# Two memory pools change places: the token sorting's tiles and the attention's weights under the recurrence's buffers

## The chip, the cores and the metric

The kernel runs on one core of a Trainium2 chip. The metric is the device time of one execution in microseconds (us), lower is better; of several runs the median is taken. The core has five engines that work side by side, each through its own instructions in a fixed order: TensorE (PE in the profile, with its weight loads as PEld), VectorE (DVE), ScalarE (ACT), GpSimd (POOL) and SyncE (SP), which here only issues DMA transfers. POOL issues the indirect DMAs (gathers and scatters of rows) and some accumulating ones. An engine waits at an instruction until the semaphores that it needs are there, and all that stands behind it on this engine waits too.

## The reference, cut to what matters

A network of four layers on x of 4 x 1024 x 128 (batch B = 4, tokens T = 1024, features D = 128), float32 throughout. After every part there is an addition of the input and a layer norm.

```
layer 0: minGRU (two levels), then a feed-forward part that goes through 64 slots
layer 1: sparse attention of 16 heads, then a gated feed-forward part
layer 2: linear attention with 16 heads of 64 (cosformer), causal;
         then experts: each token goes to its best 2 of 8
             hidden = silu(x W1[e]) * (x W3[e]);  y = sum over the 2 of p_e * (hidden W2[e])
layer 3: a selective recurrence (Mamba): 256 channels, 16 states n each
             h_n(t) = exp(delta(t) A_n) h_n(t-1) + delta(t) u(t) B_n(t)
             y(t)   = sum over n of C_n(t) h_n(t)
         then 8 experts with top-p weights: every expert is computed for every token
```

## The kernel before, in words

The program builds layer after layer (`program`, L2161 on), but a scheduler of the tile framework orders each engine's instructions over all of it: the kernel states operations and their data, the framework plans the order with its own model of costs (`TileContext(nc, schedule_with_timeline_sim=True)`) and inserts the waits. Only TensorE's order within the attention of layer 2 is written by hand (`l2_attn`), and the recurrence is put ahead of the experts of layer 2 by a raised priority (`l3`).

**Pools.** Tiles live in pools, and pools lie on two stacks, one from the left and one from the right end of each partition's memory. A pool that is opened gets the space next to the pool opened before it on its side; when it's closed, a later pool may lie over it. The first tiles of such a later pool wait until all tiles of every older pool under it have been released. This is counted by the whole pool: a tile that lies over a pool waits for that pool's last user. On the right side stand, from the end inwards, `moek` (kept values), `first`, `moet` (the experts' weights, rows and results of layer 2), and then, within the `ExitStack` called `w2`, the pool `w2` (the attention's weights wE with the constants turn, near, trig and biases) and `moed` (work tiles of the token sorting). When `w2` is closed, three pools are opened: `ssm` and `ssm2` on the left (`l3_pools`, L1679), which hold the recurrence's buffers, and `top` on the right, which holds the last layer's expert weights wh and results.

**Attention of layer 2** (L903 to L1206). TensorE projects, rotates (POOL's qt at L1059) and sums by groups of 128 tokens; its last matmul is pr (L1196, with wE), and its last norm is written by VectorE at L178 (xN).

**Token sorting** (`l2_dispatch`, L1294). For each of the four batches VectorE turns the router's ranks into target rows: prefix sums, comparisons, an index di for each choice (L1361 to L1367), a weight wt (last operation L1377). Then POOL scatters the tokens' rows to memory outside the chip: 16 indirect DMAs a batch (L1383).

**Experts of layer 2** (`l2_ffn`, L1402). The sorted tokens are worked on in 92 tiles of 128, 23 a batch, m0 to m91 here. For each tile SP loads its expert's weights wx (L1458) and its rows xg (L1442); TensorE computes ph, ScalarE and VectorE the gating (L1490 to L1494), TensorE py; ScalarE copies ys (L1510), SP stores yrows (L1512). When a batch is done, POOL gathers its rows back as yg (L1529, 16 indirect DMAs, in two halves of 8), and a norm ends the layer.

**Recurrence of layer 3** (`l3_prepare` L1718, `l3_scan` L1819). It goes over eight halves of 512 tokens (four batches, two halves each), numbered 0 to 7 here. `l3_prepare` computes xs, the rows B and C, dl (delta) and ud (delta times u, L1813) of a half. Then, for each state n from 0 to 15:

```
...
                nc.sync.dma_start(
                    out=t[:, 0, :], in_=rows[r : r + 1, :].to_broadcast([P, 512])
                )
...
            nc.gpsimd.tensor_mul(db, ud, bc[0])
...
            nc.gpsimd.tensor_mul(hc, db, bc[1])
```

SP loads the rows bn and cn to all partitions (L1844); POOL multiplies db = ud x bn (L1849); ScalarE forms da = exp (L1853); VectorE runs two scans along the tokens in place in db (L1854); ScalarE keeps the last column as carry in a first half (L1863); POOL multiplies hc = db x cn (L1865); TensorE adds hc into pys by a matmul with the identity (L127). bn, cn, db and hc have four buffers each, all in `ssm2`. When all 16 are summed, `l3_sum` and `l3_finish` (po, the norm, the router) end the half, and `l3_ffn_head` (first pgt, L1944 on) and the 8 experts of the last layer (`l3_ffn`, weights wh loaded by SP at L1677) follow for it, while POOL, VectorE and ScalarE go on with the next half.

The pools and their places in KB of a partition, before and after the change:

| pool | holds | before | after |
|---|---|---|---|
| `ssm2` (left) | bn, cn, db, hc, xnT, xs, dl, ud, tail, carry | 76.31 to 152.62 | the same |
| `moed` (right) | work tiles of the sorting | 146.81 to 156.00 | 175.88 to 185.06 |
| `w2` (right) | wE and constants of the attention | 156.00 to 185.06 | 146.81 to 175.88 |
| `top` (right) | h_acc, gT, wh, hh | 155.06 to 185.06 | the same |
| `moet` (right) | the experts' tiles of layer 2 | 185.06 to 217 | the same |

Of the kernel before, what the change touches and what calls it, by code (L numbers as in the profile page):

```python
# [49 lines left out]
def weave(*gens):  # L50

    gens = list(gens)
    while gens:
        for g in gens[:]:
            if next(g, gens) is gens:
                gens.remove(g)
# [2104 lines left out]
def program(tc, io):  # L2161
    with ExitStack() as ctx:
        n = Net(ctx, tc, io)
        wd, w0 = ExitStack(), ExitStack()
        wdp = wd.enter_context(tc.tile_pool(name="wd", bufs=1))
        W = n.l0_load(w0.enter_context(tc.tile_pool(name="w0", bufs=1)))
        d = n.l1_ffn_load(wdp)
        dp = ctx.enter_context(
            tc.tile_pool(name="rows", bufs=2, space=bass.MemoryType.DRAM)
        )  # L2170
        sd = ctx.enter_context(tc.tile_pool(name="ssmd", bufs=2, space=bass.MemoryType.DRAM))
        with ExitStack() as ff:
            last = n.front(ff, w0, W, d, dp)
            keep = ctx.enter_context(tc.tile_pool(name="moek", bufs=1, side="right"))
            first = ctx.enter_context(tc.tile_pool(name="first", bufs=1, side="right"))
            mt = ctx.enter_context(tc.tile_pool(name="moet", bufs=2, side="right"))
            w2 = ExitStack()
            n.l2_attn_load(w2.enter_context(tc.tile_pool(name="w2", bufs=1, side="right")))
            weave(*last)
        wd.close()  # L2180
        def load():
            n.l2_ffn_load()
            n.l3_load(sd)
            n.l2_rows(keep, md, dp)

        moe = n.l2_ffn(mt)
        with w2:
            md = w2.enter_context(tc.tile_pool(name="moed", bufs=1, side="right"))
            n.l2_attn(load, n.l2_dispatch, moe, first)
        n.l3_pools(ctx)  # L2190
        fp = ctx.enter_context(tc.tile_pool(name="top", bufs=2, side="right"))
        n.l3(moe, fp)
# [17 lines left out]
```

## Time and profile before

| what | us |
|---|---|
| runs | 2287.27, 2288.26, 2295.73; median 2288.26 |
| the profiled execution | 2286.79, its span 2285.0 |
| busy PE / DVE / ACT / POOL | 1978.9 / 1349.2 / 1210.5 / 1023.4 |
| attention's last pr, last norm L178 ends | 1339.7, 1345.5 |
| last operation of the last sorting (L1377) ends | 1371.4 |
| the recurrence's first bn issued, first db | 1371.5, 1390.3 |
| last hc of half 0 ends, its po begins | 1476.3, 1482.3 |
| last layer: first pgt, first expert's ph | 1545.7, 1549.1 |
| last db of the recurrence | 2134.9 |

The profile shows one execution. Its page gives busy times, the span in 40 equal slices (each digit is the busy share in tenths; PEclk is TensorE's granted clock in tenths of full speed), the chain of work that ended last, and the costliest groups of instructions. A window line gives, for a stretch of time, the busy us of each engine with its number of instructions, the granted clock, the share of time in which the 16 DMA engines were busy, and GB/s. A timeline line gives the start, the duration in us, the engine, the line of the kernel, the operation, output and inputs, the shapes, how many instructions were taken together, and in square brackets the idle time before them with what ended it. A line of waits gives an engine and an operation, whom it waited for, and the us in total, how often, and the longest.

### The profile page before, as it was taken

What the parts mean: (1) busy time and instruction counts of PE and PEld (TensorE: products, weight loads), DVE (VectorE), ACT (ScalarE), POOL (GpSimd) and SP (SyncE); (2) the same over time, 40 slices, a digit from 0 to 9 for tenths busy, and PEclk for the clock granted to TensorE, in tenths of its full rate; (3) what the DMA queues carried; (4) which work ended last, traced back from release to release, by engine and by line L of the source; (5) the groups of instructions that cost most, each with busy time, mean ns of one, the idle gap of its engine ahead of it and who ended that gap; (6) DMA issues with size and microseconds to landing.
All of it is one profiled execution on the core that took longest, in us unless ns stands there. A gap on an engine that the chain in (4) does not pass through costs nothing.

```text
span 2285.0 us, 46402 instructions
## 1 busy us (share of the span) xinstructions
PE 1978.9 (87%) x17806; PEld 1383.3 (61%) x17806; DVE 1349.2 (59%) x3693; ACT 1210.5 (53%) x2623; POOL 1023.4 (45%) x812
## 2 busy tenths in 40 slices
PE   6667979879999999999989876679899999999998
PEld 3455655444477777787767664246565656565666
DVE  6457843433355565565555555696777688776521
ACT  6543443332244444444455456576768786767443
POOL 5100230000023234224233418998889889879400
PEclk9667989979999999999999988799999999999999
DMA  3000110005000010031223147456786677776421
GB/s 107 0 14 24 30 39 1 19 10 174 1 3 2 3 35 15 17 87 49 65 80 85 37 126 221 135 175 200 216 216 178 174 189 192 193 187 167 119 61 51
DMA packets 138559, 211.10 MB, mean 92 GB/s; under 512 B 18598, under 2 KB 75937, under 8 KB 137953
## 3 DMA queue, kind: packets, MB, share of 16 engines
q1 hardware_dynamic: 126192, 173.87, 25.5%
q0 software_dynamic: 12144, 34.26, 7.1%
q8 instruction: 140, 2.29, 0.4%
q14 instruction: 83, 0.67, 0.1%
HBM read 160.29 MB, written 23.16 MB: 80 GB/s over the span
## 4 chain that ended last, share of the span: by engine, by line
PE 43%; DVE 12%; ACT 11%; issue 3%; DMA 2%; POOL 1%; SPq 0%; ACTq 0%; DVEq 0%; POOLq 0%
PE py L127 7%; PE ph L127 7%; PE po L1126 5%; PE pqk L127 5%; PE pa_m L127 5%; DVE db L1854 4%; PE pys L127 3%; PE kp_mo L127 3%; PE pv L127 2%; PE pr L1196 2%; ACT hh L1980 1%; ACT da L1853 1%; PE pt L131 1%; PE kp_mo L131 1%; ACT xN L174 1%
## 5 line engine op out<-in xcount | busy, mean ns | idle before, releaser
L1059 POOL TENSOR_TENSOR qt<-r_q,sb_c_turn 128x256 f32<-128x256 f32 (+1 forms) x256 | 164.0, 660 | 447.9 <-ACT r_q L1051 442.2
L1865 POOL TENSOR_TENSOR hc<-db,cn 128x1024 f32<-128x1024 f32 x128 | 314.7, 2493 | 57.1 <-PE pys L127 25.6
L127 PEld LDWEIGHTS py<-wh,hh 128*128 128x128 f32 x2048 | 249.8, 192 | 79.9 <-issue 44.8
L1849 POOL TENSOR_TENSOR db<-ud,bn 128x1024 f32<-128x1024 f32 x112 | 286.3, 2633 | 12.4 <-issue 9.9
L127 PE MATMUL ph<-xT,wh 128*128 128x512 f32 x512 | 256.3, 618 | 21.2 <-DVE h_acc L1996 5.8
L127 PE MATMUL py<-wh,hh 128*128 128x128 f32 x2048 | 258.2, 276 | 12.7 <-ACT hh L1980 6.6
L1980 ACT ACTIVATE hh<-ph,sb_cols 128x512 f32<-128x512 f32 x256 | 170.6, 680 | 131.1 <-PE ph L127 104.5
L1117 DVE TENSOR_TENSOR a<-pa_m,sb_c_near 128x256 f32<-128x256 f32 x256 | 96.6, 419 | 203.4 <-PE pa_m L127 203.4
L1074 ACT ACTIVATE kN<-kp_mo,sb_c_trig 128x128 f32<-128x128 f32 x448 | 129.8, 371 | 132.0 <-PE kp_mo L131 122.2
L1853 ACT ACTIVATE da<-dl,aneg 128x512 f32<-128x512 f32 x224 | 153.6, 689 | 74.4 <-DVE db L1854 73.3
L127 PE MATMUL pys<-hc,sb_c_ident 128*128 128x512 f32 x324 | 158.5, 619 | 22.7 <-POOL hc L1865 19.4
L1854 DVE TENSOR_TENSOR_SCAN db<-da,carry,db 128x512 f32<-128x512 f32 x128 | 156.9, 1265 | 11.7 <-ACT da L1853 8.8
L1854 DVE TENSOR_TENSOR_SCAN db<-da,db 128x512 f32<-128x512 f32 x128 | 149.3, 1205 | 10.4 <-POOL db L1849 6.0
L127 PEld LDWEIGHTS ph<-xT,wh 128*128 128x128 f32 x512 | 89.6, 196 | 104.7 <-issue 53.5
L1996 DVE SCALAR_TENSOR_TENSOR h_acc<-py,gt,h_acc 128x128 f32<-128x128 f32 x256 | 71.9, 342 | 125.8 <-PE py L127 125.8
L127 PE MATMUL pqk<-xT,wE 128*128 128x256 f32 x512 | 136.7, 390 | 8.3 <-ACT coT L1193 4.2
L127 PEld LDWEIGHTS pys<-hc,sb_c_ident 128*128 128x128 f32 x324 | 60.5, 199 | 86.7 <-issue 58.7
L729 POOL DMA_INDIRECT orows<-o,ix x20 | 18.9, 944 | 186.0 <-DVE o L727 160.4
L127 PEld LDWEIGHTS pqk<-xT,wE 128*128 128x128 f32 x512 | 88.5, 193 | 21.9 <-DVE cv L1036 8.1
L131 PE MATMUL pt<-sb_c_ident,xN 128*128 128x128 f32 x224 | 54.2, 345 | 51.0 <-ACT xN L174 31.8
L1193 ACT COPY coT<-pt 128x512 f32<-128x512 f32 x64 | 37.5, 586 | 114.9 <-PE pt L131 114.9
L127 PE MATMUL po<-ht,wD 128*128 128x512 f32 x192 | 93.7, 595 | 0.0
(456 smaller groups left out, 4344.1 us busy)
## 6 DMA issues: line engine op xcount, KB each, us to landing
wx<-in_wF SPq DMA_DIRECT2D x92, 384.0 KB, 3.4
bn<-rows SPq DMA_DIRECT2D x128, 256.0 KB, 5.0
cn<-rows SPq DMA_DIRECT2D x128, 256.0 KB, 4.2
wh<-in_wH SPq DMA_DIRECT2D x64, 512.0 KB, 3.8
hc<-hc POOLq DMA_DIRECT2D x47, 512.0 KB, 6.6
xrows<-zero SPq DMA_DIRECT2D x4, 1472.0 KB, 12.3
xg<-xrows SPq DMA_DIRECT2D x20, 256.0 KB, 3.0
yrows<-ys SPq DMA_DIRECT2D x20, 256.0 KB, 3.3
```

What stands on the lines that cost most here:

```text
L127: return self.nc.tensor.matmul(out=out, lhsT=lhsT, rhs=rhs, start=start, stop=stop)
L131: self.nc.tensor.transpose(out, in_, self.ident[0:n, 0:n])
L1059: nc.gpsimd.tensor_mul(u["qt"][:, m, a:], u["q"][:, a:], c2["turn"][:, m, o + a : o + 2 * P])
L1074: self.nc.scalar.activation(u["kN"][:, c, m, :], pk[:, c, :], AF.Copy, scale=trig[:, k, m : m + 1])
L1117: nc.vector.tensor_mul(u["a"][:, i, :, :], pa[i], self.c2["near"][:, None, :].to_broadcast([P, 2, P]),)
L1126: self.nc.tensor.matmul(out=u["po"][self.HALF[j], i, c, :], lhsT=lhsT, rhs=rhs, start=key not in u["begun"], stop=True, skip_group_check=True,
L1849: nc.gpsimd.tensor_mul(db, ud, bc[0])
L1853: nc.scalar.activation(da, dl[:, ec, :], AF.Exp, scale=aneg[:, j : j + 1])
L1854: nc.vector.tensor_tensor_scan(db[:, ec, :], da, db[:, ec, :], carry[:, ec, n : n + 1] if h else 0.0, ALU.mult, ALU.add,)
L1865: nc.gpsimd.tensor_mul(hc, db, bc[1])
L1980: nc.scalar.activation(ht, ph, AF.Relu, bias=self.col("h_b1", i=e * NK + k))
L1996: nc.vector.scalar_tensor_tensor(acc[:, c, :], py[:, c, :], gt[:, c, e : e + 1], acc[:, c, :], ALU.mult, ALU.add,)
```

## The change

The pool `moed` is opened before the pool `w2` instead of after it, within the same `ExitStack`; both are closed together as before.

```diff
             w2 = ExitStack()
+            md = w2.enter_context(tc.tile_pool(name="moed", bufs=1, side="right"))
             n.l2_attn_load(w2.enter_context(tc.tile_pool(name="w2", bufs=1, side="right")))
             weave(*last)
...
         moe = n.l2_ffn(mt)
         with w2:
-            md = w2.enter_context(tc.tile_pool(name="moed", bufs=1, side="right"))
             n.l2_attn(load, n.l2_dispatch, moe, first)
         n.l3_pools(ctx)
```

No operation is written differently; tiles get other addresses (the table above), and the scheduler plans the orders anew.

## The prediction

> **What bounds the kernel now.** I read the page's forty slices first, then the table of windows over the stage that the diff touches, then the lists of POOL, SP and DVE in time, then the waits of POOL and PE. The change moves memory of the last stage of the attention and of the recurrence's start, so I look for who is late there.
>
> The page's slices, three rows of them (one digit is 57 us; slices 23 to 26 are 1314 to 1542 us):
>
> ```profile
> PE   6667979879999999999989876679899999999998
> POOL 5100230000023234224233418998889889879400
> PEclk9667989979999999999999988799999999999999
> ```
>
> PE is nearly full before and after, and weak only here. The windows:
>
> ```profile
> core 0: us, PE busy (x) PEld busy (x) DVE busy (x) ACT busy (x) POOL busy (x), PEclk, DMA share, GB/s
> 1300.00:1340.00 40.00, 32.85 (x489) 27.39 (x483) 19.38 (x62) 24.22 (x52) 7.03 (x10) 0.87 0.21 64
> 1340.00:1380.00 40.00, 25.82 (x163) 23.01 (x162) 24.28 (x96) 20.38 (x54) 14.21 (x15) 0.83 0.61 177
> 1380.00:1420.00 40.00, 21.09 (x99) 16.00 (x100) 22.23 (x47) 24.64 (x60) 35.04 (x26) 0.79 0.71 230
> 1420.00:1460.00 40.00, 30.93 (x80) 14.17 (x79) 27.66 (x34) 27.26 (x50) 39.52 (x18) 0.83 0.55 156
> 1460.00:1500.00 40.00, 25.80 (x91) 14.95 (x92) 26.69 (x37) 18.49 (x35) 40.00 (x19) 0.83 0.43 129
> 1500.00:1600.00 100.00, 84.91 (x435) 56.38 (x434) 78.94 (x149) 70.66 (x146) 88.67 (x49) 0.98 0.65 193
> ```
>
> From 1420 to 1500 POOL is full (79.5 of 80 us) and PE is not (56.7): POOL bounds the start of the recurrence. From 1340 to 1380 POOL works 14.2 us only. Its list says why:
>
> ```profile
> 1323.44 1.41 POOL L1059 TENSOR_TENSOR qt<-r_q,sb_c_turn 128x256 f32<-128x256 f32 x2 [9.59 <-ACT r_q L1051]
> 1361.52 0.99 POOL L1529 DMA_INDIRECT yg<-yrows,di  x1 [36.67 <-DVE ch L1361]
> ...
> 1371.60 0.99 POOL L1383 DMA_INDIRECT xrows<-xN,di  x1 [0.30 <-DVE wt L1377]
> ...
> 1390.31 2.37 POOL L1849 TENSOR_TENSOR db<-xT,bn 128x1024 f32<-128x1024 f32 x1
> ...
> 1473.94 2.37 POOL L1865 TENSOR_TENSOR hc<-db,cn 128x1024 f32<-128x1024 f32 x1
> 1476.24 4.67 POOL L1849 TENSOR_TENSOR db<-ud,bn 128x1024 f32<-128x1024 f32 x2
> ```
>
> After 36.67 us of idleness POOL issues 8 gathers and 16 scatters of the sorted experts, starts the recurrence's first product db at 1390.31, and never rests again in half 0 (512 tokens, 16 steps), whose last hc ends at 1473.94 + 2.37 = 1476.3. Why not before 1390? The row loads bn and cn that db needs:
>
> ```profile
> 1359.24 5.58 SPq L1458 DMA_DIRECT2D wx<-in_wF  x3
> 1371.50 0.33 SPq L1844 DMA_DIRECT2D bn<-rows  x1
> ```
>
> SP issues the first bn at 1371.50, just as VectorE ends the last operation of the last sorting (L1377: 1371.18, two of 0.24 us). That is the pool wait: bn lies in ssm2, whose upper end covers the sorting's tiles (moed).
>
> **What the change does, step by step.** It swaps two pools. Before, moed lies at 146.8 to 156.0 KB of a partition and w2 (attention weights) at 156.0 to 185.1; after, w2 at 146.8 to 175.9 and moed at 175.9 to 185.1. ssm2 stays at 76.3 to 152.6, so it now lies under w2's lower end, which is wE, and no longer under moed. The order of the changed program confirms it: the first bn waits for VectorE's L178, the attention's last norm, and no more for L1377. The later pool (top, with wh) covers both in either order and still waits for the sorting. All engines' orders are the same up to about 1345 us; no operation is added or removed except two of ScalarE's function table loads.
>
> 1. *Release.* L178 ends at 1345.5 (list of VectorE: 1344.42 and four of 1.11 us in all). bn's loads take 3.0 / 4.5 / 8.9 us from issue to landing (minimum, median, maximum), so the first db can start at 1350.5 (1349 to 1355) instead of 1390.3.
>
> 2. *POOL, the only engine that counts here.* Its order up to the last hc of half 0 has, before, 32 indirect DMAs and 32 products. 28 products, 1410.83 to 1476.24, take 65.4 us, 2.336 each; an indirect DMA takes 0.96 + 0.30 = 1.26. 32 x 1.26 + 32 x 2.336 = 115.1, and the trace has 1476.3 - 1361.5 = 114.8: full without a gap. In the changed order the same 32 DMAs lie among the products, and one db of half 1 comes before the last hc: 32 x 1.26 + 33 x 2.336 = 117.4. From 1350.5 that ends at 1467.9, **8.4 us earlier** than 1476.3. So the 39.8 us that the first db moves are worth only the 11 us of idleness that POOL fills, less the one db put ahead.
>
> 3. *What hides the rest.* The 8 gathers belong to batch 1 and need its yrows stores, which SP issued at 1357.2 before; in the new order they stand after ten products, at about 1374. The 16 scatters of batch 3 end near 1434 instead of 1390; the first tile of expert work that reads them stands at about 1515 on PE, so 80 us of other tiles hide it. The sorting on VectorE now shares its time with four scans (L1854, 2 x 1.24 us a step, 9.9 us in all): 25.3 us of VectorE work between the last norm and the sorting's first index instead of 15.4. That makes the index late by about 10 us, 1370 to 1380; the first scatter stands on POOL at 1350.5 + 11 x 2.336 + 8 x 1.26 = 1386. Cover 6 us; without it POOL stands still behind the scatter by whatever is missing.
>
> 4. *SP.* Eight row loads now stand ahead of, and nine more among, the expert weights wx (L1458) of tiles 46 to 52, and those that wait for a bn or cn buffer to come free hold back the wx behind them. By adding the rows I get these wx 4 to 9 us later. PE has the room: from 1340 to 1500 it is idle 56 of 160 us (103.6 busy in the table's four rows). If the cover is gone, PE's accumulations pys of the recurrence, which stand behind these tiles in PE's order, come late, hc's four buffers stay taken and POOL stops: up to the same 4 to 9 us.
>
> 5. *From half 0 to the end.* fin (PE at 1482.26), head (pgt, 1545.73) and the first expert of the last layer (1549.06) follow half 0 with the same work and nearly the same PE order, so they move with it. After 1550 PE is the pacemaker (85 to 96% busy), with idle time in short pieces; POOL's waits name PE (25.6 us at L1865, 1476 to 2140), PE's name POOL's accumulating DMAs with 3.2 us only. So the shift is neither multiplied nor, as the same PE work is still to be done behind it, eaten: 1 : 1. I take -8.4; bounds are 0 (all given back) and -11 (idle filled, the extra db hidden).
>
> *Two rules against the rows.* The products that now start at 1350 run beside a VectorE that has sorting and scans to do (25.3 us of work where 15.4 were, point 3). In 1410 to 1476 a product takes 2.336 us; the later ones of half 1 on (L1849, 112 of them) take 2.633 on the page, so a product costs up to 0.30 more beside other neighbours: 33 x 0.30 = 9.8, which would take the whole gain. I keep 2.336, as VectorE was 55 to 69% busy there too, and keep 9.8 for the range. The Trainium skill (SBUF — State Buffer, "Who interferes with whom") says that a VectorE instruction with two SBUF inputs and a GpSimd instruction that reads SBUF exclude each other for a whole instruction. Taken strictly it speaks against this change, since the sorting is full of such instructions; as they are short (0.24 us at L1377) and about ten products lie beside them, it would by my estimate cost some 2.4 us.
>
> The clock: the same group of 8 ph takes 1.13 us in a run of work and 2.05 us after an idle 9.87 us (1388.46), and the granted clock is 0.79 to 0.83 from 1340 to 1500 against 0.98 behind. The Trainium skill (TensorE: Matmul & The Clock Gate, "What's actually happening") says that an idle window of some 3.4 us halves the clock. Filled idleness on PE would be worth double by that rule; PE doesn't set the end of this stage, so I count nothing.
>
> **The profiled execution against the median.** It took 2286.8 us (span 2285.0) and the runs' median is 2288.3. 2288.3 - 8.4 = 2279.9, predicted 2280. Half a per cent, about what a measurement of this kernel can tell from no change, is 11.4 us: under 2276.8 is faster, over 2299.7 slower.
>
> **Cases.**
>
> *Forecast* (0.44): -3 to -14, as above. The limit of 2276.8 is at -11.4; about 0.10 of this case lies beyond it.
>
> *A. More comes* (0.22): the shift also lets the tail in. PE is idle 132 us between 1340 and 2285, 57 of them after 1548. In the new order the last pys of the recurrence stands some 10 us of PE work earlier among the last layer's experts, so its closing chain (sum, norm, router) is covered by more of them. -8.4 - 10 = -18, to -26: 2262 to 2270. For it: POOL is idle in the last two slices of the page, so that chain lies bare of it. Against it: PE is 96.5 of 100 us busy in 2100 to 2200, so there's little to win.
>
> *B. Nothing comes* (0.14): ud of half 1 decides. Its delta projection pd now stands after the ninth pys on PE. By adding rows ud is ready at 1460 and its first db stands at 1461.5: before, ud was done at 1446.0 (L1813) for a db at 1476.2, 30 us of slack; now 1.5. If VectorE or PE is 8 us late, half 1 starts where it did; or the products take 2.633. 2284 to 2290.
>
> *C. Slower* (0.20): the row loads on SP stop POOL. From the fifth step on, a bn or cn load waits in SP's queue until POOL gives a buffer back, and wx stand behind it; the tiles of these wx stand on PE ahead of the pys that free the four hc buffers; POOL's next hc waits for such a buffer and so holds the db behind it. The place is tiles 46, 49 and 52, ahead of the pys of steps 0, 4 and 8, between 1375 and 1440. A hold costs 4 to 9 us (point 4). One is less than the 8.4 us won; it decides from two full ones on, and three are 27 - 8.4 = +18.6: 2290 to 2307. For it: wx is already what PE's ph waits for in 1280 to 1500 (17.1 us, 6 times), at a DMA share of 0.61 to 0.71. Against it: PE's 56 idle us, and that by the rows each hc has 1 to 10 us of slack.
>
> *That the change doesn't do what it says* is excluded by the new wait of the first bn.
>
> **Chances.** Faster by over 0.5%: 0.10 + 0.22 = 0.32. Slower: C beyond +11.4, 0.15, and 0.02 for B beyond its bounds: 0.17. Between: 0.51. The range 2262 to 2297 takes in A, B and the lower half of C; some 0.18 is left out.
>
> **What would show it.** Right: first bn issued at 1346, first db at 1349 to 1355, POOL without gaps over 2 us until the last hc of half 0 at 1466 to 1470, fin near 1474, head near 1537. Wrong: stops of POOL between 1350 and 1468 with hc or xrows named as waiting for VectorE or PE (C); half 0 early, first db of half 1 late for ud (B); products over 2.5 us before 1468; head early by 8 and the end not, which breaks point 5.

## The result, and the profile after

| what | before | after |
|---|---|---|
| runs side by side, median (20 each) | 2289.81 | 2296.39 |
| ratio, 95% interval | | 1.0027 [1.0014, 1.0039] |
| profiled execution, its span | 2286.79, 2285.0 | 2295.22, 2293.5 |
| DVE busy in the span | 1349.2 | 1363.0 |
| attention's last norm ends (L178) | 1345.5 | 1346.5 |
| first bn issued, first db | 1371.5, 1390.3 | 1346.6, 1350.6 |
| last sorting ends (L1377) | 1371.4 | 1389.4 |
| last hc of half 0 ends | 1476.3 | 1476.1 |
| last hc of half 4 ends | 1870.9 | 1877.4 |
| last hc of half 7 ends | 2146.8 | 2151.7 |

The changed kernel is 6.6 us, 0.27%, slower. The recurrence does start 39.7 us earlier, but half 0 ends where it ended before, and behind that 8.7 us are lost (817.4 us from there to the end of the span instead of 808.7), which the prediction had not counted. The rows of the page that answer to the three shown of before:

```profile
PE   6667979879999999999979867689898989898998
POOL 5100230000123235234243338989789889789400
PEclk9767989979999999999999988889999999999999
```

POOL has work in slice 23 now, but PE's late slices alternate between 8 and 9 where nearly all were 9. The windows of after:

```profile
core 0: us, PE busy (x) PEld busy (x) DVE busy (x) ACT busy (x) POOL busy (x), PEclk, DMA share, GB/s
1340.00:1380.00 40.00, 22.83 (x120) 19.19 (x119) 31.02 (x53) 20.00 (x50) 23.11 (x10) 0.71 0.65 201
1380.00:1420.00 40.00, 31.37 (x145) 22.08 (x143) 32.34 (x87) 23.09 (x62) 34.51 (x27) 0.86 0.76 227
1420.00:1460.00 40.00, 24.59 (x80) 14.01 (x81) 20.92 (x35) 25.15 (x49) 36.82 (x24) 0.79 0.48 142
1460.00:1500.00 40.00, 27.76 (x101) 15.24 (x100) 32.85 (x53) 23.38 (x43) 38.38 (x18) 0.87 0.47 144
```

In the first window POOL does 23.11 us of work instead of 14.21, as wanted. But VectorE is busy 31.02 us with 53 instructions where it was 24.28 us with 96: fewer and longer, eight of them scans of some 1.17 us that weren't there before. From 1380 to 1460 POOL doesn't stop: what it lacks there to full windows are the 0.16 to 0.31 us ahead of each of its indirect DMAs. Its stops lie before and behind that stretch. POOL's list of after, here its start and the three longest stops of half 0 (the brackets hold the idle time and what is named as ending it):

```profile
1350.60 6.97 POOL L1849 TENSOR_TENSOR db<-xT,bn 128x1024 f32<-128x1024 f32 x3 [24.83 <-PE py L127]
1357.50 2.37 POOL L1865 TENSOR_TENSOR hc<-db,cn 128x1024 f32<-128x1024 f32 x1
1359.80 2.41 POOL L1849 TENSOR_TENSOR db<-xT,bn 128x1024 f32<-128x1024 f32 x1
1362.18 2.79 POOL L1865 TENSOR_TENSOR hc<-db,cn 128x1024 f32<-128x1024 f32 x1
1368.50 2.65 POOL L1865 TENSOR_TENSOR hc<-db,cn 128x1024 f32<-128x1024 f32 x1 [3.53 <-DMA bn<-rows]
...
1376.32 2.35 POOL L1865 TENSOR_TENSOR hc<-db,cn 128x1024 f32<-128x1024 f32 x1 [2.76 <-ACT da L1853]
...
1466.82 2.36 POOL L1865 TENSOR_TENSOR hc<-db,cn 128x1024 f32<-128x1024 f32 x1 [1.62 <-DMA cn<-rows]
```

The three stops are 3.53 + 2.76 + 1.62 = 7.9 us (7.9 to 8.1 us in all five traces of the changed kernel). The first one is put down to a bn load, but an hc reads db and cn and not bn: it starts at 1368.50, 0.12 us behind the scans of its step, which VectorE ran at 1366.05 for 2.33 us. Why these came so late is in VectorE's list of after:

```profile
1358.53 1.42 DVE L1238 TENSOR_TENSOR rt_p<-rt_l,rt_m 128x64 f32<-128x64 f32 x1
1359.88 1.21 DVE L1854 TENSOR_TENSOR_SCAN db<-da,db 128x512 f32<-128x512 f32 x1
1361.01 1.75 DVE L1246 TENSOR_TENSOR rt_q<-rt_p 128x512 f32<-128x512 f32 x1
1362.69 2.83 DVE L1250 TENSOR_TENSOR rt_g<-rt_p 128x512 f32<-128x512 f32 x1
...
1366.05 2.33 DVE L1854 TENSOR_TENSOR_SCAN db<-da,db 128x512 f32<-128x512 f32 x2
...
1370.13 1.08 DVE L1304 TENSOR_SCALAR sel<-rt_r 128x64 f32<-128x64 f32 x1
1371.13 2.47 DVE L1361 TENSOR_SCALAR ch<-rt_r 128x64 f32<-128x64 f32 x2
...
1373.86 2.32 DVE L1854 TENSOR_TENSOR_SCAN db<-da,db 128x512 f32<-128x512 f32 x2
...
1376.73 1.96 DVE L1289 COPY inc<-cnt 128x8 f32<-128x8 f32 x1
```

The same operations in before, where POOL stood idle beside them:

```profile
1355.07 0.22 DVE L1238 TENSOR_TENSOR rt_p<-rt_l,rt_m 128x64 f32<-128x64 f32 x1
1355.32 0.69 DVE L1246 TENSOR_TENSOR rt_q<-rt_p 128x512 f32<-128x512 f32 x1
1355.93 0.69 DVE L1250 TENSOR_TENSOR rt_g<-rt_p 128x512 f32<-128x512 f32 x1
...
1360.48 0.19 DVE L1304 TENSOR_SCALAR sel<-rt_r 128x64 f32<-128x64 f32 x1
1360.58 0.29 DVE L1361 TENSOR_SCALAR ch<-rt_r 128x64 f32<-128x64 f32 x2
...
1363.00 0.17 DVE L1289 COPY inc<-cnt 128x8 f32<-128x8 f32 x1
```

These operations of the sorting take from 2.5 to 12 times as long beside POOL's products: L1250 starts at 1362.69, the product at 1362.18 ends at 1364.97, and L1250 ends at 1365.52, 0.55 us later; alone it takes 0.69. The scans took 1.16 to 1.21 us each; they have one input in PSUM (da). The waits nearly make up the first two stops: L1246 and L1250 took 3.2 us more than in before, ahead of the scans of the first stop (3.53 us), and L1304 and the pair at L1361 3.1 us more, ahead of those of the second (2.76 us).

The third stop is another one. The sorting had ended at 1389.4; the scans that the hc at 1466.82 needs stand behind the preparation of half 1:

```profile
1463.33 0.42 DVE L1491 SCALAR_TENSOR_TENSOR sg<-sg,ph 128x256 f32<-128x256 f32 x1 [1.70 <-ACT sg L1490]
1463.67 0.69 DVE L1812 TENSOR_TENSOR pd<-sp_w,pd 128x512 f32<-128x512 f32 x1
1464.27 2.33 DVE L1854 TENSOR_TENSOR_SCAN db<-da,db 128x512 f32<-128x512 f32 x2
```

The theory for the first two, then: *VectorE's sorting operations wait out whole products; the scans stand behind them in VectorE's order, and POOL's hc behind the scans.* Rivals: the row loads are what stops POOL (case C, and the name in the first bracket); or the old order was simply the better one; and for the loss behind half 0: the order there, one gate operation in it, or the clock.

### The profile page after: what moved, and what is told of

Its sections match the earlier page's. It is cut to its first block, busy times and chain, and to the rows that moved or that the text cites. A ratio compares the mean times of both kernels' runs of the same rounds, so it can differ in the third digit from the quotient of the medians.

```text
span 2293.5 us, 46368 instructions
## 1 busy us (share of the span) xinstructions
PE 1987.4 (87%) x17806; PEld 1392.6 (61%) x17806; DVE 1363.0 (59%) x3693; ACT 1208.8 (53%) x2621; POOL 1025.5 (45%) x812
## 4 chain that ended last, share of the span: by engine, by line
PE 44%; DVE 13%; ACT 9%; issue 3%; DMA 2%; POOL 1%; SPq 0%; ACTq 0%; DVEq 0%; POOLq 0%
PE py L127 8%; PE ph L127 7%; PE po L1126 5%; DVE db L1854 5%; PE pqk L127 5%; PE pa_m L127 4%; PE pys L127 3%; PE kp_mo L127 3%; PE pv L127 2%; PE pr L1196 2%; PE pt L131 1%; ACT hh L1980 1%; PE kp_mo L131 1%; ACT da L1853 1%; DMA hc<-hc 1%
## 5 line engine op out<-in xcount | busy, mean ns | idle before, releaser
L127 PEld LDWEIGHTS py<-wh,hh 128*128 128x128 f32 x2048 | 255.9, 196 | 82.2 <-issue 44.5
L127 PE MATMUL py<-wh,hh 128*128 128x128 f32 x2048 | 263.7, 280 | 15.0 <-ACT hh L1980 9.8
L1074 ACT ACTIVATE kN<-kp_mo,sb_c_trig 128x128 f32<-128x128 f32 x448 | 130.2, 372 | 131.8 <-PE kp_mo L131 122.0
L127 PE MATMUL pys<-hc,sb_c_ident 128*128 128x512 f32 x324 | 167.2, 642 | 17.5 <-POOL hc L1865 12.3
L1854 DVE TENSOR_TENSOR_SCAN db<-da,db 128x512 f32<-128x512 f32 x128 | 149.4, 1205 | 11.3 <-ACT da L1853 6.7
```

What stands on the lines that cost most here:

```text
L127: return self.nc.tensor.matmul(out=out, lhsT=lhsT, rhs=rhs, start=start, stop=stop)
L1074: self.nc.scalar.activation(u["kN"][:, c, m, :], pk[:, c, :], AF.Copy, scale=trig[:, k, m : m + 1])
L1854: nc.vector.tensor_tensor_scan(db[:, ec, :], da, db[:, ec, :], carry[:, ec, n : n + 1] if h else 0.0, ALU.mult, ALU.add,)
```

## The experiments

The runs fell on five chips. In the runs above and on two of the chips the kernel before takes 2289 us; on three it takes 2330 to 2337 us, and the changed kernel gains there. So each ratio is to the kernel before on its own chip, and runs are compared within a chip. All times below come from the profiled executions and are counted from the end of the attention's last norm, to the last hc of half 0, for half 4 alone (last hc of half 3 to last hc of half 4), and from the last hc of half 3 to the end of the span.

| run | before there | ratio [95%] | half 0 ends | half 4 | half 3 to end |
|---|---|---|---|---|---|
| (the kernel before, first profile) | | | 130.8 | 93.0 | 507.1 |
| (the changed kernel, first profile) | 2289.8 | 1.0027 [1.0014, 1.0039] | 129.6 | 98.6 | 514.6 |
| before_again | 2336.5 | 0.9997 [0.9980, 1.0014] | 142.7 | 92.6 | 507.0 |
| after_again | 2336.5 | 0.9938 [0.9912, 0.9965] | 129.6 | 101.4 | 511.7 |
| rows_wait | 2336.5 | 1.0037 [1.0017, 1.0056] | 138.5 | 108.5 | 521.7 |
| sort_psum | 2336.5 | 0.9893 [0.9870, 0.9916] | 118.3 | 98.5 | 508.7 |
| after_2 | 2335.2 | 0.9942 [0.9921, 0.9963] | 129.6 | 101.3 | 510.7 |
| half1_wait | 2335.2 | 0.9928 [0.9906, 0.9950] | 128.9 | 92.9 | 506.7 |
| sort_scan | 2335.2 | 0.9904 [0.9883, 0.9926] | 118.1 | 100.1 | 510.2 |
| wh_late | 2335.2 | 0.9999 [0.9981, 1.0018] | 141.7 | 92.2 | 504.9 |
| after_3 | 2289.0 | 1.0033 [1.0017, 1.0049] | 129.6 | 98.3 | 513.4 |
| scan_old_pools | 2289.0 | 1.0005 [0.9989, 1.0022] | 129.9 | 92.7 | 507.1 |
| scatter_late | 2289.0 | 1.0076 [1.0053, 1.0099] | 133.4 | 108.2 | 522.0 |
| sort_scan_2 | 2289.0 | 0.9998 [0.9986, 1.0010] | 118.5 | 100.7 | 510.8 |
| after_4 | 2288.8 | 1.0042 [1.0027, 1.0056] | 129.3 | 98.6 | 514.8 |
| gate_behind | 2288.8 | 1.0021 [1.0008, 1.0034] | 130.6 | 98.1 | 511.8 |
| half1_wait_2 | 2288.8 | 0.9990 [0.9978, 1.0002] | 129.0 | 92.2 | 505.0 |
| scan_half1 | 2288.8 | 1.0007 [0.9993, 1.0022] | 118.4 | 100.7 | 511.0 |
| scan_half3 | 2330.3 | 1.0042 [1.0021, 1.0062] | 118.2 | 112.3 | 531.4 |
| half1_wait_3 | 2330.3 | 0.9937 [0.9917, 0.9957] | 130.2 | 92.7 | 503.9 |

### Is it the release alone?

`before_again` and `after_again` are the two kernels once more, as measures. `rows_wait` is the changed kernel with the first four steps' row loads held until the last sorting is done. That was to give back the order of the kernel before with the changed kernel's addresses; but the planner made a third order of it. In its trace some 85 of POOL's 812 instructions and 977 of VectorE's 3693 stand elsewhere than in before, from 1361 us on.

```diff
-            nc.vector.tensor_mul(v, v, sm)
+            self.sorted = nc.vector.tensor_mul(v, v, sm)
...
+                if b == h == 0 and n < 4:
+                    self.tc.add_manual_dep(i.ins, self.sorted.ins.name, SYNC, reason="after the sorting")
```

> The kernel before once more, for a second profile and the scatter. Every theory: 2290 us within its runs' spread. In the profile half 0 ends at 1476, and TensorE's time at half clock behind 1500 (half of each half-clock stretch) tells what is the order's and what is chance: if the order of instructions decides, about 15 us are lost again as in the first profile; if it is chance, anything from 10 to 25.

> The changed kernel once more. Every theory: 2296 us (ratio 1.002 to 1.004). Theory 'port' (sorting's operations on VectorE wait for whole products on POOL, the scans stand behind them, and POOL's hc behind these): the first db at 1350, L1250 again 2 to 3 us instead of 0.69, half 0 ends at 1475 to 1477. If the loss behind 1800 is the new order's own, po of half 6 is 8 to 13 us later than in before_again and half-clock losses behind 1500 are about 25 us; if chance, they fall to 15.

> The changed pools, but the first four bn and cn loads wait for the sorting's last operation: new addresses, and every engine's order as before the change. Theory 'port and order': time as before, 2290 (ratio 0.998 to 1.002), L1250 0.69 us. Rival 'addresses' (w2 and moed at other places cost something by themselves): 2296, ratio 1.003.

On this chip the changed kernel won 0.6%, and with the loads held back the gain was gone: 1.0037. That fits a change that works through the early loads, but doesn't show it, as the order differs too. VectorE now has the recurrence's xc (L1759 on) and a norm of the experts (L157) among the sorting's operations, and the sorting ends 36.3 us behind the attention's norm instead of 26.8; halves 1 and 4 take 110.4 and 108.5 us instead of 99.0 and 92.6 in `before_again`. That other addresses cost time by themselves is not excluded by this run.

### Does VectorE wait out the products?

`sort_psum` lets the last batch's sorting keep its logits, its ranks and one table of comparisons in PSUM, so that its large operations have one input in SBUF instead of two. Their number is the same, and SP's loads aren't touched; the planner orders all engines anew, as in every build.

```diff
+        if rb:
+            v = ps([P, 3, n * NE], "prl").rearrange("p i (c e) -> p i c e", e=NE)
+            pl, lg, pp = v[:, 0], v[:, 0], v[:, 1]
+            q = rb([P, n * NE, NE], "prq").rearrange("p (c e) j -> p c e j", e=NE)
...
-        rank = tile("r", NE)
+        rank = v[:, 2] if rb else tile("r", NE)
```

> The changed kernel, and in the last batch's sorting the probabilities, the rank matrix, the ranks and offsets lie in PSUM, so that most of its VectorE operations have one SBUF input at most. Theory 'port': L1246, L1250 and L1361 fall back to 0.3 to 0.7 us beside the products, and half 0 ends 4 to 8 us earlier (1468 to 1472); the time is then 2283 to 2292, depending on whether the later loss of 6 us stays. Rival 'VectorE is simply full' (scans and sorting need the time anyway): the durations of those lines may fall but half 0 still ends at 1475 to 1477 and the time stays at 2296.

Half 0 ended 118.3 us behind the norm, 11.3 us before the changed kernel's 129.6. VectorE's list of `sort_psum` (the comparisons that were L1246 and L1250 are L1250 and L1254 here):

```profile
1383.13 0.67 DVE L1250 TENSOR_TENSOR prq<-rt_p,prl 128x512 f32<-128x512 f32 x1
1383.71 0.68 DVE L1254 TENSOR_TENSOR rt_g<-rt_p,prl 128x512 f32<-128x512 f32 x1
...
1389.12 0.21 DVE L1369 TENSOR_SCALAR ch<-prl 128x64 f32<-128x64 f32 x1
...
1392.46 4.46 DVE L1293 COPY inc<-cnt 128x8 f32<-128x8 f32 x1
```

and POOL's beside it:

```profile
1382.89 2.41 POOL L1857 TENSOR_TENSOR db<-xT,bn 128x1024 f32<-128x1024 f32 x1
1385.24 2.37 POOL L1873 TENSOR_TENSOR hc<-db,cn 128x1024 f32<-128x1024 f32 x1
...
1389.89 4.66 POOL L1873 TENSOR_TENSOR hc<-db,cn 128x1024 f32<-128x1024 f32 x2
1394.51 2.39 POOL L1857 TENSOR_TENSOR db<-xT,bn 128x1024 f32<-128x1024 f32 x1
```

The comparisons are back at 0.67 and 0.68 us in the middle of products. What was left in SBUF still waits, and worse: a copy of 8 elements starts at 1392.46, in the second of three products that follow each other without a gap, and ends at 1396.92, just behind the third (1394.51 + 2.39 = 1396.90). It took 4.46 us instead of 0.17.

`sort_scan` takes these away as well: the counts by expert lie side by side and the two prefix sums are one scan each, with an input in PSUM, instead of copies and additions.

```diff
+            inc = turn(pp[:, 3])
+            nc.vector.tensor_tensor_scan(pp[:, 3], m2["first"], pp[:, 1], 0.0, ALU.mult, ALU.add)
...
-            inc = self.prefix(wp, tot, NC, "inc")
```

`scan_old_pools` is the control: the same shorter sorting with the pools in the order of before. `after_2`, `after_3` and `sort_scan_2` repeat two kernels as measures beside others.

> The changed kernel a third time, since it came out at 1.0027 of before in the first measurement and at 0.994 in the second, where all times were 2% longer. If the ratio goes with the overall time: about 0.994 where before takes some 2335 us, about 1.003 where it takes some 2290. Half 0 ends 129 to 130 us after the attention's last norm (129.6 in both profiles so far).

> As sort_psum, and the prefix sums of the last batch's sorting are two scans instead of twelve copies and additions, and the casts read PSUM: nearly no operation of this sorting has two SBUF inputs or copies from SBUF to SBUF any more. Theory 'port': no VectorE operation of the sorting takes over 1 us, the last index is ready 25 to 30 us after the last norm (47 in sort_psum), and half 0 ends 115 to 119 us after the norm (118.3 in sort_psum, 129.6 in after): ratio to before 0.985 to 0.992 where before takes 2335, 0.994 to 1.000 where it takes 2290. Rival 'VectorE is full anyway': half 0 ends 125 us or more after the norm.

> The changed kernel once more, as the measure for the three others. 0.994 of before where before takes some 2335 us, 1.003 where it takes some 2290; half 0 ends 129 to 130 us after the attention's last norm.

> The sorting of sort_scan with the pools of before. Theory 'port': the products start only behind the sorting here, so nothing blocks it anyway, and only its fewer operations count: last index 3 to 6 us earlier than the 24 us after the norm of before, half 0 earlier by as much, ratio 0.997 to 0.999. Rival 'the gain of sort_scan is its shorter sorting and has nothing to do with the pools': ratio as sort_scan, 0.990.

> sort_scan once more beside after_3. Theory 'port': 0.3 to 0.5% faster than after_3 wherever it runs, since half 0 ends 11 us earlier in both: 0.990 where before takes 2335, 0.998 where it takes 2290.

Half 0 ends at 118.1 and 118.5. The last index comes 37 us behind the norm and not 25 to 30, as expected, which costs POOL nothing. The last operation with two SBUF inputs still took 4.00 us (L1396, in `sort_scan_2`), ahead of a scatter that POOL issued 0.17 us after its last product. POOL's first products of `sort_scan_2`:

```profile
1346.57 7.01 POOL L1871 TENSOR_TENSOR db<-xT,bn 128x1024 f32<-128x1024 f32 x3 [25.18 <-DMA bn<-rows]
...
1371.27 0.96 POOL L1551 DMA_INDIRECT yg<-yrows,di  x1 [0.31 <-issue]
```

Between these and up to 1384 POOL's list has no idle time but the 0.31 us between indirect DMAs. With the shorter sorting and the old pools, half 0 ends at 129.9 and the time is 1.0005: the shorter sorting alone is worth nothing (with POOL idle beside it, it ends 25.1 us behind the norm instead of 25.9). Both together end half 0 11 us ahead of the changed kernel and 12 us ahead of the kernel before, and POOL has no stop left. Of the 11 us 7.9 are the stops and 2.3 a db of half 1 that no longer stands ahead of the last hc. With no edit to SP's loads the stops are gone, so the row loads were not their cause. The order of instructions changed in these builds as well; that the locks made the first two stops, and not the order alone, rests on the rows above. The times follow, by less than half 0: 0.9998 beside 1.0033 where the kernel before takes 2289 us, 0.9904 beside 0.9942 and 0.9893 beside 0.9938 where it takes 2335 (these two pairs of intervals just touch). More than half of the gain is lost in half 1 already: its first db, which now waits for its ud, starts 122.9 us behind the norm in `sort_scan_2` (122.6 in after), 4.4 us after half 0's end, and half 1 takes 101.5 us instead of 95.4 in `after_3`. It ends 5 us earlier, where half 0 ended 11 us earlier. That is the mechanism of case B in the prediction. Against the kernel before nothing is left at the end: 0.9998.

### What is lost behind half 3

In all five traces of the changed kernel half 4 takes 98.3 to 101.4 us, against 92.2 to 93.0 in the kernel before, `scan_old_pools` and `wh_late`. VectorE's list of after, at the start of half 4:

```profile
1785.36 0.16 DVE L168 SCALAR_TENSOR_TENSOR ln_nm<-pmv,ln_rs 128x4 f32<-128x4 f32 x1
1790.31 0.69 DVE L1901 SCALAR_TENSOR_TENSOR th<-th,psk 128x512 f32<-128x512 f32 x1 [4.79 <-ACT th L1900]
1790.92 4.56 DVE L1854 TENSOR_TENSOR_SCAN db<-da,db 128x512 f32<-128x512 f32 x4
```

and POOL's:

```profile
1785.90 3.10 POOL L1849 TENSOR_TENSOR db<-ud,bn 128x1024 f32<-128x1024 f32 x1
1793.38 4.68 POOL L1865 TENSOR_TENSOR hc<-db,cn 128x1024 f32<-128x1024 f32 x2 [4.38 <-issue]
```

The gate of half 3 (L1901) waits 4.79 us for ScalarE, and half 4's first scans stand behind it. In before they stand ahead:

```profile
1787.61 2.33 DVE L1854 TENSOR_TENSOR_SCAN db<-da,db 128x512 f32<-128x512 f32 x2
1792.07 1.22 DVE L1854 TENSOR_TENSOR_SCAN db<-da,db 128x512 f32<-128x512 f32 x1 [2.14 <-ACT da L1853]
1793.21 0.66 DVE L1901 SCALAR_TENSOR_TENSOR th<-th,psk 128x512 f32<-128x512 f32 x1
```

`gate_behind` moves that one operation behind the first two scans; every other engine's order stays. `half1_wait` holds half 1's first db until half 0's last hc, as it was in the kernel before, and thereby the planner takes nearly the old order again from there on (26 of POOL's 302 instructions behind half 0 stand elsewhere than in before, 197 in after).

```diff
+            if b == 2 and h == n == 0:
+                self.tc.add_manual_dep(self.behind().ins, scan.ins.name, SYNC, reason="scans first")
```

```diff
+            if b == 0 and h == 1 and n == 0:
+                self.tc.add_manual_dep(i.ins, self.last.ins.name, SYNC, reason="after half 0")
...
+            self.last = nc.gpsimd.tensor_mul(hc, db, bc[1])
```

> The changed kernel, but the first db of half 1 waits for the last hc of half 0, so that it can't go ahead of it on POOL; the orders behind come out anew. Theory 'POOL goes ahead too far' (B in the prediction): ud and half 1 are not what decides, so half 0 ends at the same distance and the time is that of after_2 within 0.2%. Rival 'the new order behind half 0 costs the time': the time moves by 0.2% or more against after_2, to either side, though nothing in half 0 got faster.

> The changed kernel once more, as the measure of the three beside it. Every theory: half 0 ends 129.6 us behind the attention's last norm; half 4 takes 98 to 102 us (98.6, 98.3, 101.4 and 101.2 in the four traces so far); 511 to 515 us from the end of half 3 to the end of the kernel.

> The changed kernel with one thing moved: the second gate operation of half 3 (L1901) stands behind the first two scans of half 4 on VectorE instead of ahead of them; every other engine's order is as in the changed kernel. If the gate ahead of the scans is what half 4 loses: GpSimd's stop of 4.4 us at the head of half 4 goes, half 4 takes 93 to 95 us, 507 to 510 us from the end of half 3 to the end, and the time is 4 to 6 us (0.2 %) under the changed kernel's of this call. If the rest of the new order or the half-clock stretches are what it loses: the stop goes or not, half 3 to the end stays 511 to 515 us, and the time stays within 2 us of the changed kernel's.

> The changed kernel with half 1's first product held until half 0's last one, which gives half 1 on GpSimd the order that the kernel before has. The order of the pieces decides: half 4 takes 93 us (92.9 in this kernel's first trace), half 3 to the end 506 to 508 us, as in the kernel before, and the time is 4 to 7 us under the changed kernel's. The clock decides and not the order: half 3 to the end 511 to 515 us and the time within 2 us of the changed kernel's.

> The changed kernel with half 1's first product held until half 0's last one, a third time, as the measure beside the one above. If the order of half 1 and what follows from it is the second loss: half 4 takes 92 to 93 us, half 3 to the end 505 to 507 us, the time is 0.998 to 1.0005 of the kernel before on a chip where that takes 2289 us (0.9928 where it takes 2335 us). If its second run was chance: 511 to 515 us and 1.002 to 1.004.

`gate_behind`: POOL's stops at the head of half 4, 4.38 and 0.81 us, became these two, 2.86 and 0.89:

```profile
1794.39 2.36 POOL L1867 TENSOR_TENSOR hc<-db,cn 128x1024 f32<-128x1024 f32 x1 [2.86 <-DVE db L1854]
1797.64 2.36 POOL L1867 TENSOR_TENSOR hc<-db,cn 128x1024 f32<-128x1024 f32 x1 [0.89 <-DVE db L1854]
```

Half 4 still took 98.1 us. The gate alone is not it; the third scan is still behind it. Half 3 to the end came down by 3 us to 511.8, short of the 507 to 510 expected, and the intervals of 1.0021 and 1.0042 overlap. `half1_wait` brings half 4 back to 92.2 to 92.9 on three chips and half 3 to the end to 503.9 to 506.7. Where the kernel before takes 2289 us it has 0.9990 beside the changed kernel's 1.0042, 10 us, and the intervals are apart. So on such a chip the loss comes from the order that follows on half 1. Where it takes 2335 us the time moved by 0.14% only (0.9928 beside 0.9942), less than the 0.2% expected, and the intervals overlap. The clock goes along with the order in half 4; a window line of after, and of `half1_wait_2`:

```profile
1780.00:1880.00 100.00, 89.78 (x424) 57.28 (x425) 76.69 (x158) 77.97 (x146) 84.41 (x42) 0.98 0.65 175
```

```profile
1780.00:1880.00 100.00, 93.34 (x446) 58.61 (x445) 80.98 (x158) 84.56 (x156) 89.36 (x46) 1.00 0.71 192
```

With the new order every engine does less in these 100 us, and the granted clock is 0.98 instead of 1.00; with the order undone both return. Over the whole stretch from 1500 to 2285 us the granted clock is 0.98 in before and `half1_wait_2` and 0.97 in after, `after_3` and `after_4`; but on the other chips it is 0.97 in `before_again`, 0.96 in `half1_wait` and 0.96 in `after_again`, so there it doesn't go with the order. Whether the slower clock is a part of the loss or only follows the pauses, these runs don't tell.

`scan_half1` adds the held half 1 to the shorter sorting; `scan_half3` holds half 3's first db until half 2's last hc there.

```diff
-            if b == 0 and h == 1 and n == 0:
+            if (b, h, n) == (1, 1, 0):
```

> The sorting shortened (its operands in PSUM, two scans for its prefix sums) and, besides, half 1's first product held until half 0's last one. If the two losses are separate, they add up: half 0 ends 118 us behind the norm (11 us before the changed kernel's) and half 3 to the end is 506 to 508 us, so that the time is 12 to 18 us under the changed kernel's, some 0.4 % under the kernel before on the chip where that takes 2289 us. If the order behind half 3 follows from when half 0 ends, holding half 1 changes nothing there: half 3 to the end 510 us, and the time is that of the kernel with the shortened sorting alone, 8 us under the changed kernel's.

> The shortened sorting, with half 3's first product held until half 2's last one. In this build GpSimd's order in half 3 (seven of its eight gathers and four products ahead of the last two pieces) and at the start of half 4 is that of the kernel before. If a half's own order sets its length: half 4 takes 92 to 94 us (100.7 in the shortened sorting's own order), and with half 0's end at 118 us the time is 6 to 12 us under the kernel before, 0.9948 to 0.9974 of it on a chip where that takes 2289 us. If the late halves lose whatever their order once half 0 ends earlier: half 4 stays near 100 us, half 3 to the end 510 us, and the time is 0.998 to 1.001 of the kernel before, as the shortened sorting alone had.

The first changed nothing: half 0 ends at 118.4 there, and half 1's first db follows at 123.0 in any case, as it waits for ud. Behind half 0 POOL, VectorE, ScalarE and SP have the order of `sort_scan`, so it is that kernel once more (half 4 takes 100.7 us), and whether the two losses are separate stays open. The second is a miss for both theories. In letters (d a db, h an hc, a an accumulating DMA; each row ends with the half's sixteenth hc), POOL's order of half 4 as built:

```
before, half1_wait  adddadhhhdhaddadhhhdhaddadhhhdhaddadhhhh
after, sort_scan    dddadhhhdhaddadhhhdhaddadhhhdhaddadhhhdh
scan_half3          adddadhhhdadhdhadhdhadhdhadhdhadhdhadhhaddh
```

`scan_half3` begins half 4 as before does, and then goes a third way, with a stop of 8.76 us at its head and 112.3 us in all. That a half's first pieces on POOL settle its length is refuted. The rows of "after" and "before" differ in little: the first accumulation falls ahead of the half, and one db of half 5 stands ahead of the last hc. That db waits for its ud besides:

```profile
1872.76 2.36 POOL L1849 TENSOR_TENSOR db<-ud,bn 128x1024 f32<-128x1024 f32 x1 [1.90 <-DVE ud L1813]
```

POOL's stops of more than 0.2 us in half 4 sum up to 15.6 us in after and 11.4 in before. These 4.2 us (1.90 of them this wait) and 2.35 for the db, less some 0.9 for the accumulation, are the 5.6 us between 98.6 and 93.0. Which instructions on the other engines make the remaining stops is open.

### The chips where the kernel before takes 2335 us

There half 0 of the kernel before ends 142.7 us behind the norm instead of 130.8; the changed kernel's 129.6 is the same on both. POOL in `before_again` stands still for VectorE, where the first profile of before has one stop of 0.48 us in half 0:

```profile
1443.48 9.43 POOL L1849 TENSOR_TENSOR db<-xT,bn 128x1024 f32<-128x1024 f32 x4
1461.24 6.97 POOL L1865 TENSOR_TENSOR hc<-db,cn 128x1024 f32<-128x1024 f32 x3 [8.33 <-DVE db L1854]
```

My theory was the burst of wh loads, which in before falls together with the row loads and the scatters. `wh_late` holds three of them back in the kernel before; `scatter_late`, also made from the kernel before, puts one scatter behind each hc.

```diff
+            if i < 3:
+                self.tc.add_manual_dep(j.ins, self.late.name, SYNC, reason="not in the burst")
```

```diff
+                if hasattr(self, "last"):
+                    self.tc.add_manual_dep(i, self.last.name, SYNC, reason="one behind each hc")
```

> The kernel before, but the first three loads of wh (0.5 MB each) wait for the ninth hc of half 0 instead of being issued right behind the sorting's end, in the middle of the row loads and the wx. Theory 'burst' (where before takes 2335, transfers that all start at the sorting's end starve TensorE of wx, and that is what the change takes away there): half 0 ends 3 to 10 us earlier than in before_again (142.7 us after the norm), ratio 0.996 to 0.999; where before takes 2290 it is 1.000. Rival: ratio 1.000 or above in both.

> The kernel before, but each of the last batch's 16 scatters waits for an hc of half 0, so they no longer fall together with the first row loads. Theory 'scatters beside row loads': in the profiles with 2335 us VectorE, ScalarE and TensorE stand still together for 7 to 9 us while POOL issues these scatters, and SP needs 1.42 us for a load instead of 0.46; without the scatters there half 0 ends 131 to 137 us after the norm instead of 142, ratio 0.995 to 0.998. Rival (something else stalls them): the stall stays, 140 or more, ratio 1.000 or above.

`wh_late` changed nothing (141.7 us, 0.9999): that theory falls. `scatter_late` fell on a chip without the effect, so it says nothing on it; there it was 1.0076, with other orders behind (half 3 to the end 522.0). Why these chips are slower with the late start of the recurrence stays open.

## Why the prediction was wrong

It gave 2280 us with a range to 2297, and the changed kernel took 2296.4; the direction was wrong. That 2296.4 lies under the range's upper end is luck: the end was put there for case C, whose mechanism didn't come. (The prediction's chances also don't agree there: with 0.15 of C's 0.20 beyond 2299.7, a range to 2297 takes in a quarter of C at most, and not its lower half.) In the two profiled executions the spans moved by +8.5 us instead of -8.4. Of these 16.9 us 7.2 arose in half 0, which ends 1.2 us earlier from the norm and not 8.4 (point 2), 8.7 behind it (point 5), and 1.0 ahead of the norm.

1. *Release*: right. First bn at 1346.59, first db at 1350.60, against 1350.5 worked out.
2. *POOL*: **the step that failed is "full without a gap" carried over to the new order.** The terms held (a product takes 2.34 to 2.79 us, an indirect DMA 1.26), but POOL stopped for 7.9 us in three pieces, 6.3 behind the sorting's locked operations and 1.6 behind half 1's preparation: 117.4 + 7.9 = 125.3, and the trace has 1476.1 - 1350.6 = 125.5. The term that was mis-sized is the exclusion of VectorE by POOL's products, put at 2.4 us; it measured 11.3 on VectorE (below). With the lock mostly taken away in `sort_scan`, half 0 takes 114.5 us from its first db, beside 115.1 worked out for 64 pieces. So the sum was right for a POOL that nothing holds, and at the end of half 0 the 8.4 us are there to be had. No run carried them to the end of the kernel: against before, `sort_scan_2` has 0.9998 and `scan_half1` 1.0007.
3. *What hides the rest*: the last sorting ended 18.0 us later (1389.4), its first index came 15 us later, and 10 were counted. The scatters were ready for POOL nevertheless: no stop ahead of one is over 0.31 us, since the stops had set POOL back as well.
4. *SP and case C*: POOL did stop, but not by C's mechanism; with no edit to SP's loads the stops went.
5. *1 : 1*: failed too. From half 3 to the end the changed kernel takes 513.4 to 514.8 us on the chips where before takes 2289 us, instead of 507.1; half 1 starts 7 us ahead of half 0's end, the planner orders all that follows anew, and that order was worse by 6 to 8 us. `half1_wait` undoes that part and shows what the change is worth without it: 0.9990 [0.9978, 1.0002].

*The two rules against the rows.* The prediction weighed the rule of the Trainium skill (SBUF — State Buffer, "Who interferes with whom") and put it at 2.4 us. The rows say: seven lines of VectorE's list (L1238, L1246, L1250, L1304, the pair at L1361 and two at L1289) took 13.8 us where they took 2.4 in before, so 11.3 us were waited. The mistake was in the working: the sorting's operations were taken to be short and so cheap to exclude. It is the other side that is long: a 0.17-us copy waits for the rest of a 2.3-us product. The page also names copies, casts and tensor_scalar in their two-port modes as ones that exclude GpSimd, and the rows agree: the copy at L1289 (1.96 us), the pair at L1361 (2.47), and in `sort_psum` a cast of 8 elements (L1375 there, 4.32 us instead of 0.15). It says as well that who issues first holds the ports; that a waiting instruction can also be passed over by GpSimd's next product is shown by the copy's 4.46 us. And the scans, with one input in PSUM, weren't held themselves (1.16 to 1.21 us each): POOL's 6.3 us came from their standing behind the sorting. The clock, which the prediction counted at nothing, had no gain to give: from 1340 to 1500 the windows have 0.71, 0.86, 0.79 and 0.87 granted, where before has 0.83, 0.79, 0.83 and 0.83.

Cases A and B didn't come in the changed kernel: half 1's first db started at 1469.1, 1.0 us behind its ud (1468.1), so case B's condition was close, but POOL didn't wait for it. With the shorter sorting it did.

## What to carry to other kernels

Before moving GpSimd's work under VectorE's, look which of VectorE's instructions there have both inputs in SBUF, or copy small pieces within it: each may wait for the rest of a GpSimd instruction, however short it is itself, and all that stands behind it in VectorE's order waits too; one input in PSUM took that away here. Where a planner orders the instructions, a local gain isn't carried to the end 1 : 1: the order behind may cost as much as the gain, and pinning one dependency to its old place can show how much. Look also at what the next stage waits for: here half 1 could start no earlier, as its ud wasn't ready, and more than half of what half 0 had gained was lost. A change worth a few tenths of a per cent may have another sign on another chip; here it was +0.3% to +0.4% on one kind and -0.6% on the other.

## What the runs showed of the hardware

The same program took 2289 us on some chips and 2330 to 2337 on others, 2% more, and not evenly. Of the 49.4 us between the profiles of before and `before_again` 22.0 arose ahead of the attention's last norm, 11.9 in half 0, 15.6 in halves 1 to 3, and none behind (507.1 and 507.0 us). In half 0 SP needed 8.2 us to issue the first eight row loads instead of 4.8 (the last four 1.43 us apart); the changed kernel's half 0 takes 129.6 us on both kinds. A VectorE instruction that waits beside GpSimd isn't always let in between two products that follow each other without a gap: 4.46 us for a copy of 8 elements per partition, 4.00 us for L1396 of `sort_scan_2`; in the changed kernel a copy at 1376.73 was let in after 1.96 us.
